# Graph attention with residual norms: the last half blocks' norms moved to VectorE, one residual added through TensorE

## The chip, the cores and the metric

The kernel runs on one core of a Trainium2 chip. A core has TensorE (matrix products, written PE in the profile; PEld is its loading of weights), VectorE (DVE), ScalarE (ACT), GpSimd (POOL) and SyncE (SP), which issues most of the transfers. The metric is the device time of one execution in microseconds (us), as the median of several runs.

## The reference

There are 8 graphs of 2048 nodes with 256 channels, and one 2048 x 2048 adjacency matrix for all. One attention layer with 8 heads of 32 channels is computed, then a feed-forward part, with three layer norms (the two inside have a gain and an offset):

```python
qkv = einsum('fnc,ck->fnk', x, w_qkv); q, k, v = split(qkv, 3)      # 8 heads of 32
scores = where(adj > 0, q @ k.T / sqrt(32), -1e9)
t = softmax(scores) @ v
y = layernorm(x + t, ln1_g, ln1_b)
h = relu(y @ w1 + b1)
z = layernorm(y + h @ w2 + b2, ln2_g, ln2_b)
out = layernorm(x + z)          # over the 256 channels, no gain or offset
```

All of it is in float32. The outputs are 8 x 2048 x 256 numbers.

## The kernel before

**Items.** The work is cut into items (f, qc, g, mb): graph f, a block qc of 512 queries (four to a graph), a group g of four heads, and a block mb of 128 keys. Graphs are the outer loop, then query blocks, the two groups, and 16 key blocks. For each item `scores` does the score products of TensorE (L276) into PSUM and two mask adds of VectorE (L279, operation TENSOR_TENSOR p<-s,mask), `exponentials` one ACTIVATE of ScalarE over 128 x 2048 numbers (L283), and `values` the products with v (L310). `add_up` (L330 to L339) sums the exponentials of the key blocks, partly with adds on GpSimd and partly with accumulating DMAs that GpSimd issues. The loop issues the exponential of item t + 1, the scores of item t + 2 and the values of item t in step t. A score buffer is free for the next product when VectorE has read it; there are three pairs of PSUM banks for scores, and two banks more, one for the values in progress and one for everything else.

**Side work.** Everything else is written as generators that are kept in the list `fill`, each with a start step and a due step. In every step `advance` resumes those that are ready, ordered by due step. `yield n` means: not before n steps from now. `yield BANK` waits for the free PSUM bank, of which there is one a step as long as values are being accumulated, and it is also held back by a credit for TensorE's time. So what a generator issues between two yields lands on every engine's queue at that place of the order. Each engine works through its queue in order.

For one query block the side work is: `denominator` (L382) adds up the four remaining terms with products against `halves`; `outcome` then takes the transposed values (`divide`, L427), multiplies by the reciprocals, adds the input rows x and starts `tail`. `tail` is norm, `feed_forward` (transposes, L575, w1 with L588, w2 with the add L601), norm, gain g2 and offset be2 on GpSimd (L441, L443), the residual of the input, norm, and the output DMA (L449). `norm` takes statistics on VectorE (L348, L349), four small operations on GpSimd (L353 to L357) for the reciprocal deviation rs and the bias nb, and four ACTIVATE on ScalarE (L360).

**The end.** Three query blocks from the end are special. For block NCK - 3 of the last graph the usual form is used with a due step that is nearer. For block NCK - 2 the input rows `xb` lie in SBUF already, and L411 adds them to y on VectorE; everywhere else an accumulating DMA (L414) does that. Its second residual, too, comes from `xb`, to which be2 has been added (L435), as the operand of L443. This block is called the third block or the block in front below. The very last group of heads, ENDING, is worked through in two halves of 256 queries (h = 0 and 1), each with eight items of two key blocks; its score products are L264, its mask adds L268, its values L298 with the copy L303. For each half `closing(h)` is started: five denominator terms (L490; the list `terms` says which sum and the earliest step), the add into dT (L493), transposes, reciprocal (L504), products with it (L522), the input rows (L525), a norm (`half_stats`, L456 to L460, and `half_norm`), transposes, L537, w1 with L545, w2 with the add L555, a second norm, g2 and be2 with the residual (L560, L561), a third norm, and the output DMA (L565). GpSimd computes the residual path beside it (L531, L532). The norm itself is, before the change,

```python
nc.vector.scalar_tensor_tensor(nb, mv[:, :, 0], -1.0, rs, op0=ALU.mult, op1=ALU.mult)
for j in range(2):
    nc.scalar.activation(t[:, j, :], t[:, j, :], AF.Identity, bias=nb[:, j:j + 1], scale=rs[:, j:j + 1])
```

After the last item `advance` is called until `fill` is empty, and the order in which the two closings and the third block's tail alternate comes out of that. A last check of the sums (L971 to L982) follows; on these inputs the branch after it isn't taken.

Of the kernel before, what the change touches and what calls it, by code (L numbers as in the profile page):

```python
# [10 lines left out]
F32 = mybir.dt.float32  # L11
# [4 lines left out]
AF = mybir.ActivationFunctionType  # L16
ALU = mybir.AluOpType
AX = mybir.AxisListType

P = 128  # L20
# [9 lines left out]
BANK, MORE, WAIT, TURNED, ROOM, INPUTS = -1, -2, -3, -4, -5, -10  # L30
# [21 lines left out]
def in_columns(nc, out, lhsT, rhs, start, stop):  # L52
    for r in range(0, P, D):
        nc.tensor.matmul(out[r:r + D], lhsT[:, r:r + D], rhs, start=start, stop=stop)  # L54
# [7 lines left out]
def fast_path(ctx, tc, cst, x, adj, out, RS):  # L62
    nc = tc.nc
    F, N, C = x.shape
    NCK, TPC, MB = N // CH, CH // P, N // P
# [12 lines left out]
    small = ctx.enter_context(tc.tile_pool(name="small", bufs=4))  # L78
# [6 lines left out]
    ident, identb, wqkv, w1s, w2s = cst["ident"], cst["identb"], cst["wqkv"], cst["w1s"], cst["w2s"]  # L85
    state = {"pair": 0, "side": None, "turn": 0, "turned": False, "holder": None, "tails": 0, "credit": 0}

    def columns(out, lhsT, rhs, start, stop):
        state["credit"] -= 4 * out.shape[-1]
        in_columns(nc, out, lhsT, rhs, start, stop)  # L90
# [11 lines left out]
    def bank(dt=F32):  # L102
        shape = [P, CH] if dt == F32 else [P, 2, CH]
        if state["side"] is not None:
            i = 1 - state["side"]
            return ps_x[i].tile(shape, dt, name=f"x{i}")
        i = state["turn"]
        state["turn"] = (i + 1) % 5
        pool = ps_s[i] if i < 3 else ps_x[i - 3]
        return pool.tile(shape, dt, name=f"s{i}" if i < 3 else f"x{i - 3}")  # L110
# [4 lines left out]
    def take(shape, dt):  # L115
        live.pop(0)
        live.append(ld.tile(shape, dt, name="in"))
        return live[-1]
# [245 lines left out]
    def rows(v):  # L364
        return v[:, None, :].to_broadcast([P, TPC, C])
# [35 lines left out]
    def outcome(f, qc):  # L401
        yield ROOM
        state["tails"] += 1
        xin = x[f, qc * CH:(qc + 1) * CH, :].rearrange("(p j) c -> p j c", p=P)
        y = yp.tile([P, TPC, C], F32, name="y")
        begin = items.index((f, qc, 1, LAST)) + SUM + 2
        yield from divide(f, qc, y)
        if (f, qc) == (F - 1, NCK - 2):
            yield 1
            xb = state["xb"]  # L410
            nc.vector.tensor_tensor(y, y, xb, ALU.add)  # L411
            start(begin + 3, tail(f, qc, y, xin, 2, xb), begin + 18)
            return
        nc.gpsimd.dma_start(y, xin, accum_op=ALU.add)  # L414
        if (f, qc) == (F - 1, NCK - 3):
            start(begin + 10, tail(f, qc, y, xin, 2), begin + 18)
        else:
            start(begin + 10, tail(f, qc, y, xin), begin + 26)

    def divide(f, qc, y):  # L420
        rc = RC.pop((f, qc))
        for gg in range(2):
            oT = OT.pop((f, qc, gg))
            yield BANK
            ps = bank()
            transposes(ps, [oT[:, j::TPC] for j in range(TPC)])
            nc.vector.tensor_tensor(y[:, :, gg * P:(gg + 1) * P].rearrange("p j (h d) -> p j h d", d=D),  # L427
                                    ps.rearrange("p (j h d) -> p j h d", h=4, d=D),
                                    rc[:, :, gg::2, None].to_broadcast([P, TPC, 4, D]), ALU.mult)

    def tail(f, qc, y, xin, per=1, xb=None):
        yield from norm(y, per)
        yield from feed_forward(y)
        if xb is not None:
            nc.gpsimd.tensor_tensor(xb, xb, rows(cst["be2r"]), ALU.add)  # L435
        yield 1
        z = y
        yield from norm(z, per if per == 1 else TPC)
        while xb is None and per > 1 and state["now"] % MB not in CALM:
            yield 1  # L440
        nc.gpsimd.tensor_tensor(z, z, rows(cst["g2r"]), ALU.mult)  # L441
        yield 1
        nc.gpsimd.tensor_tensor(z, z, rows(cst["be2r"]) if xb is None else xb, ALU.add)  # L443
        yield 1
        if xb is None:
            nc.gpsimd.dma_start(z, xin, accum_op=ALU.add)
            yield 7 if per == 1 else 10
        yield from norm(z, per)
        nc.sync.dma_start(out[f, qc * CH:(qc + 1) * CH, :].rearrange("(p j) c -> p j c", p=P), z)  # L449
        state["tails"] -= 1  # L450

    def half_stats(t):
        mv = small.tile([P, 2, nc.vector.BN_AGGR_DIM], F32, name="mv")
        for j in range(2):
            st = small.tile([P, nc.vector.BN_STATS_DIM], F32, name="st")
            nc.vector.bn_stats(st, t[:, j, :])  # L456
            nc.vector.bn_aggr(mv[:, j, :], st)
        rs = small.tile([P, 2], F32, name="rs")
        nc.gpsimd.tensor_scalar(rs, mv[:, :, 1], EPS, 1.0, op0=ALU.add, op1=ALU.mult)
        nc.gpsimd.tensor_tensor(rs, rs, cst["mhalf"][:, 0:2], ALU.pow)  # L460
        return mv, rs

    def half_norm(t, mv, rs):
        nb = small.tile([P, 2], F32, name="nb")
        nc.vector.scalar_tensor_tensor(nb, mv[:, :, 0], -1.0, rs, op0=ALU.mult, op1=ALU.mult)
        for j in range(2):
            nc.scalar.activation(t[:, j, :], t[:, j, :], AF.Identity, bias=nb[:, j:j + 1], scale=rs[:, j:j + 1])

    def closing(h):
        f, qc, g = ENDING  # L470
# [4 lines left out]
        def row2(v):  # L475
            return v[:, None, :].to_broadcast([P, 2, C])

        yield BANK
        ps = bank()
        for n, (block, when) in enumerate(terms):  # L480
# [6 lines left out]
            for b in range(2):  # L487
                for i in range(4):
                    r = D * i
                    nc.tensor.matmul(ps[r:r + D, 0:HQ], cst["halves"][:, g, :], term[:, i, b * HQ:(b + 1) * HQ],  # L490
                                     start=(n + b == 0), stop=(n + b == len(terms)))
# [6 lines left out]
        xr, xb = (t[:, own] for t in state["rows"])  # L498
# [27 lines left out]
        found = half_stats(y)  # L526
        if h:
            count(den)
        yield 1
        half_norm(y, *found)  # L530
        nc.gpsimd.tensor_tensor(xr, y, row2(cst["g1r"]), ALU.mult)  # L531
        nc.gpsimd.tensor_tensor(xr, xr, row2(cst["be1b2r"]), ALU.add)  # L532
        yield BANK
        ps = bank()
        transposes(ps, [y[:, j, a * P:(a + 1) * P] for a in range(2) for j in range(2)])
        for a in range(2):
            nc.scalar.activation(yT[:, a, part], ps[:, a * HQ:(a + 1) * HQ], AF.Identity,  # L537
                                 bias=cst["be1c"][:, a:a + 1], scale=cst["g1c"][:, a:a + 1])
        yield 1
        for d in range(2):  # L540
            yield BANK
            ps = bank()
# [5 lines left out]
        ps = bank()  # L548
# [4 lines left out]
                columns(ps[:, j * C:(j + 1) * C], hT[:, d, part][:, j * P:(j + 1) * P], w2s[:, d, :], start=(d == 0), stop=(d == 1))  # L553
        z = y
        nc.vector.tensor_tensor(z, ps.rearrange("p (b c) -> p b c", c=C), xr, ALU.add)  # L555
        found = half_stats(z)
        yield 1
        half_norm(z, *found)
        yield 1
        nc.vector.tensor_tensor(z, z, row2(cst["g2r"]), ALU.mult)  # L560
        nc.vector.tensor_tensor(z, z, xb, ALU.add)  # L561
        found = half_stats(z)
        yield 1
        half_norm(z, *found)
# [41 lines left out]
    def start(t, gen, due):  # L606
        fill.append([t, gen, 1, due])
        fill.sort(key=lambda e: e[3])
# [120 lines left out]
    for t, (f, qc, g, mb) in enumerate(items):  # L729
# [17 lines left out]
        if t == len(items) - MB:  # L747
            xr, xb = state["rows"] = [take([P, TPC, C], F32) for _ in range(2)]
# [23 lines left out]
    t = len(items)  # L772
# [244 lines left out]
```

## Time and profile before

| what | value |
|---|---|
| median of 3 runs | 3167.66 us (3167.57 to 3168.4) |
| profiled execution | 3165.28 us |
| its span, first to last instruction | 3163.5 us |
| granted TensorE clock, mean | 0.995 |
| busy: TensorE, VectorE, ScalarE, GpSimd | 97%, 87%, 77%, 82% |
| L279, mask add 128 x 1024 | 2016 of 1218 ns |
| L283, exponential 128 x 2048 | 1024 of 1910 ns |
| L339, GpSimd's add 128 x 2048 | 378 of 4881 ns |
| L411, the add of `xb` | one of 5009 ns |
| last scores of the last item begin | 3115.66 us |
| last output DMA issued after | 3158.23 us |

Times inside the span are counted from its first instruction. A line of the profile names the engine, the operation and the tiles (output <- inputs), and L with a number is the line of the kernel's file. A bracket at the end of a timeline row gives the time that the engine had been idle, and the instruction that ended this. In the timeline a duration covers an instruction's own latency: neighbours on one engine overlap by about a tenth of a microsecond, so the time from start to start is what counts for sums.

### The profile page before, as it was taken

Reading aid. Unit: us, or ns where it says so; the run is one execution under the profiler, and the core shown is the slowest. Engines: PE = TensorE matmul, PEld = TensorE weight load, DVE = VectorE, ACT = ScalarE, POOL = GpSimd, SP = SyncE. Lnnn points to the kernel's source line nnn. Section 1 sums busy time; section 2 is a strip of 40 time slices with the busy share of each in tenths; the row PEclk is TensorE's granted clock in tenths of the full one; section 3 lists DMA queues with packets and bytes.
Section 4 is the critical chain, followed back from the end, with each engine's and each line's share of the span. In section 5 each row is a group of like instructions: output and inputs, shape, how many; then the busy total and the mean of one; then the engine's idle time right before and its main releaser. Section 6 shows DMA issues by size and latency. Waiting matters only on the chain.

```text
span 3163.5 us, 68998 instructions
## 1 busy us (share of the span) xinstructions
PE 3071.6 (97%) x29220; PEld 969.5 (31%) x29220; DVE 2751.4 (87%) x3138; ACT 2423.8 (77%) x1934; POOL 2589.8 (82%) x1358
## 2 busy tenths in 40 slices
PE   8899999999999999999999999999999999999986
PEld 4222233222332233322333323323233323332223
DVE  4989888998888998888988898888888888889885
ACT  4777777777778877778877878777778777778774
POOL 1768888888888988888888888888889888889885
PEclk9999999999999999999999999999999999999998
DMA  8998888988888988789878888879879888888861
GB/s 255 224 213 187 189 184 182 205 189 192 178 176 202 198 186 182 167 197 218 186 168 187 191 199 192 180 174 204 193 172 205 178 192 193 177 174 167 174 149 42
DMA packets 165467, 586.89 MB, mean 186 GB/s; under 512 B 15360, under 2 KB 84480, under 8 KB 116512
## 3 DMA queue, kind: packets, MB, share of 16 engines
q0 software_dynamic: 63696, 430.60, 69.0%
q1 hardware_dynamic: 100640, 150.50, 14.1%
q8 instruction: 231, 3.78, 0.5%
q10 hardware_dynamic: 816, 1.31, 0.1%
q14 instruction: 84, 0.69, 0.1%
HBM read 146.15 MB, written 37.75 MB: 58 GB/s over the span
## 4 chain that ended last, share of the span: by engine, by line


## 5 line engine op out<-in xcount | busy, mean ns | idle before, releaser
L279 DVE TENSOR_TENSOR p<-s,mask 128x1024 f32<-128x1024 f32 x2016 | 2371.1, 1218 | 302.3 <-PE s L276 170.2
L283 ACT ACTIVATE p<-p 128x2048 f32<-128x2048 f32 x1024 | 1955.8, 1910 | 565.3 <-DVE p L279 458.2
L339 POOL TENSOR_TENSOR p<-p 128x2048 f32<-128x2048 f32 x378 | 1845.1, 4881 | 332.7 <-ACT p L283 332.2
L276 PE MATMUL s<-qT,kT 32*128 32x512 f32 x8064 | 1152.4, 640 | 48.1 <-DVE p L279 44.7
L310 PE MATMUL x<-p,v 128*32 128x512 f32 x8064 | 1075.3, 605 | 3.0 <-ACT oT L314 3.0
L276 PEld LDWEIGHTS s<-qT,kT 32*128 32x128 f32 x8064 | 315.5, 183 | 653.6 <-DVE p L279 627.7
L336 POOL DMA_DIRECT2D p<-p x378 | 406.5, 1076 | 69.7 <-ACT p L283 49.4
L310 PEld LDWEIGHTS x<-p,v 128*32 128x32 f32 x8064 | 158.7, 108 | 768.2 <-issue 303.5
L382 PE MATMUL x<-p,halves 128*32 128x512 f32 x2016 | 261.1, 592 | 0.3 <-ACT turned L575 0.3
L54 PE MATMUL x<-in,wqkv 128*32 128x512 f32 x1888 | 245.6, 592 | 1.5 <-DVE y L170 0.8
L360 ACT ACTIVATE y<-y,nb,rs 128x256 f32<-128x256 f32 x372 | 218.3, 591 | 1.5 <-POOL nb L357 1.4
L348 DVE BATCH_NORM_STATS2 st<-y 128x6 f32<-128x256 f32 x372 | 154.7, 416 | 0.0
L54 PE MATMUL x<-turned,w1s 128*32 128x512 f32 (+1 forms) x1024 | 127.1, 593 | 0.0
L54 PEld LDWEIGHTS x<-wqkv,in 128*32 128x32 f32 x3584 | 102.2, 110 | 62.9 <-issue 54.5
L54 PE MATMUL x<-w2s,hT 128*32 128x256 f32 x2016 | 120.3, 379 | 0.0
L54 PE MATMUL x<-wqkv,in 128*32 128x128 f32 x3584 | 117.1, 273 | 0.0
L382 PEld LDWEIGHTS x<-p,halves 128*32 128x32 f32 x2016 | 65.4, 110 | 149.8 <-issue 147.2
L54 PEld LDWEIGHTS x<-in,wqkv 128*32 128x32 f32 x1888 | 61.1, 110 | 143.4 <-issue 115.1
L354 POOL TENSOR_TENSOR rs<-rs,mhalf 128x4 f32<-128x4 f32 x93 | 96.2, 1035 | 7.7
L441 POOL TENSOR_TENSOR y<-y,g2r 128x1024 f32<-128x1024 f32 x31 | 100.4, 3240 | 0.0
L443 POOL TENSOR_TENSOR y<-y,be2r 128x1024 f32<-128x1024 f32 x30 | 92.1, 3071 | 0.6
L54 PEld LDWEIGHTS x<-w2s,hT 128*32 128x32 f32 x2016 | 65.4, 110 | 68.9 <-issue 35.3
(155 smaller groups left out, 1423.1 us busy)
## 6 DMA issues: line engine op xcount, KB each, us to landing
p<-p POOLq DMA_DIRECT2D x380, 1024.0 KB, 10.1
in<-xd SPq DMA_DIRECT2D x87, 512.0 KB, 8.7
mask<-md SPq DMA_DIRECT2D x248, 128.0 KB, 8.5
y<-in_x_dram POOLq DMA_DIRECT2D x60, 512.0 KB, 9.7
out_dram<-y SPq DMA_DIRECT2D x31, 512.0 KB, 5.9
in<-in_x_dram SPq DMA_DIRECT2D x30, 512.0 KB, 10.3
xd<-in SPq DMA_DIRECT2D x28, 512.0 KB, 8.3
p<-in_adj_dram SPq DMA_DIRECT2D x8, 1024.0 KB, 14.1
```

Of the source, the lines that this page charges most:

```text
L54: nc.tensor.matmul(out[r:r + D], lhsT[:, r:r + D], rhs, start=start, stop=stop)
L276: nc.tensor.matmul(ps2[half][:, j, :], KT[f, mb // TPC, g][r:r + D, (mb % TPC) * P:(mb % TPC + 1) * P], QT[f, qc, g][r:r + D, :], start=Tr ...
L279: nc.vector.tensor_tensor(pt[:, 2 * half:2 * half + 2, :], ps, MK[f, qc, mb // 2][:, mb % 2, None, :].to_broadcast([P, 2, CH]), ALU.add)
L283: nc.scalar.activation(PT[item], PT[item], AF.Exp, scale=1.0 / math.sqrt(D))
L310: nc.tensor.matmul(O[grp][r:r + D, :], V[f, mb // TPC, g][:, mb % TPC, r:r + D], PT[item][:, h, :], start=(mb == 0), stop=(mb == LAST))
L336: nc.gpsimd.dma_start(PT[f, qc, g, chain[0]], PT.pop(item), accum_op=ALU.add)
L339: nc.gpsimd.tensor_tensor(first, first, PT.pop(item), ALU.add)
L348: nc.vector.bn_stats(st, t[:, j, :])
L354: nc.gpsimd.tensor_tensor(rs, rs, cst["mhalf"], ALU.pow)
L360: nc.scalar.activation(t[:, j, :], t[:, j, :], AF.Identity, bias=nb[:, j:j + 1], scale=rs[:, j:j + 1])
L382: nc.tensor.matmul(ps[r:r + D, :], cst["halves"][:, g, :], term[:, h, :], start=(n == 0), stop=(n == len(blocks) - 1))
L441: nc.gpsimd.tensor_tensor(z, z, rows(cst["g2r"]), ALU.mult)
```

## The change

Three things are changed. In `outcome` the input rows of the third block are no longer added by L411: for two halves of the block, TensorE multiplies the identity matrix with two rows' worth of `xb` into a PSUM bank, VectorE adds that bank to y, and `tail` starts at begin + 4 instead of begin + 3. In `tail`, for this block alone, the two `yield 1` around the second GpSimd step (L443) go. In `closing` the norms are done by VectorE alone: `half_norm` becomes one `tensor_scalar` for each of two rows, subtracting the mean and multiplying by rs, without nb; and the second norm is put together with g2 and the residual in two steps for each row, the first of which needs only the mean.

```diff
         if (f, qc) == (F - 1, NCK - 2):
-            yield 1
             xb = state["xb"]
-            nc.vector.tensor_tensor(y, y, xb, ALU.add)
-            start(begin + 3, tail(f, qc, y, xin, 2, xb), begin + 18)
+            for j in range(0, TPC, 2):
+                yield BANK
+                ps = bank()
+                columns(ps, ident, xb[:, j:j + 2, :].rearrange("p j c -> p (j c)"), start=True, stop=True)
+                nc.vector.tensor_tensor(y[:, j:j + 2, :], ps.rearrange("p (j c) -> p j c", c=C), y[:, j:j + 2, :], ALU.add)
+            start(begin + 4, tail(f, qc, y, xin, 2, xb), begin + 18)
             return
...
         nc.gpsimd.tensor_tensor(z, z, rows(cst["g2r"]), ALU.mult)
-        yield 1
+        if xb is None:
+            yield 1
         nc.gpsimd.tensor_tensor(z, z, rows(cst["be2r"]) if xb is None else xb, ALU.add)
-        yield 1
         if xb is None:
+            yield 1
             nc.gpsimd.dma_start(z, xin, accum_op=ALU.add)
...
     def half_norm(t, mv, rs):
-        nb = small.tile([P, 2], F32, name="nb")
-        nc.vector.scalar_tensor_tensor(nb, mv[:, :, 0], -1.0, rs, op0=ALU.mult, op1=ALU.mult)
         for j in range(2):
-            nc.scalar.activation(t[:, j, :], t[:, j, :], AF.Identity, bias=nb[:, j:j + 1], scale=rs[:, j:j + 1])
+            nc.vector.tensor_scalar(t[:, j, :], t[:, j, :], mv[:, j, 0:1], rs[:, j:j + 1], op0=ALU.subtract, op1=ALU.mult)
...
         nc.vector.tensor_tensor(z, ps.rearrange("p (b c) -> p b c", c=C), xr, ALU.add)
-        found = half_stats(z)
-        yield 1
-        half_norm(z, *found)
-        yield 1
-        nc.vector.tensor_tensor(z, z, row2(cst["g2r"]), ALU.mult)
-        nc.vector.tensor_tensor(z, z, xb, ALU.add)
+        mv, rs = half_stats(z)
+        for j in range(2):
+            nc.vector.scalar_tensor_tensor(z[:, j, :], z[:, j, :], mv[:, j, 0:1], cst["g2r"], op0=ALU.subtract, op1=ALU.mult)
+        yield 1
+        for j in range(2):
+            nc.vector.scalar_tensor_tensor(z[:, j, :], z[:, j, :], rs[:, j:j + 1], xb[:, j, :], op0=ALU.mult, op1=ALU.add)
         found = half_stats(z)
         yield 1
         half_norm(z, *found)
```

In the changed file the line numbers are shifted by two or three from `outcome` on: the adds of the identity products are L414 with the products under `in_columns` (L54), `half_norm` is L469, and the two new steps of the second norm are L560 and L563. Where the prediction speaks of rows that both kernels have, it uses the numbers of the kernel before.

## The prediction

> **What bounds the kernel now.** I read the page first. In its busy table TensorE has 97% of the span, and the 40 slices are even up to the last. The two built programs issue the same order on every engine until about 3042 us of the span of 3163.5, so only the last 125 us can differ. The page's chain of waits is empty for this execution, so I read those from the timeline, engine by engine, then the stage table of that stretch for the granted clock.
>
> First the third residual (`state["xb"]`, L411), which the change replaces. Timeline, columns: start us, duration us, engine, line and operation, idle before it and what ended that:
>
> ```profile
> 3042.45 0.68 DVE L427 TENSOR_TENSOR y<-x,rc 128x512 f32<-128x512 f32 x1
> 3043.05 2.34 DVE L279 TENSOR_TENSOR p<-s,mask 128x1024 f32<-128x1024 f32 x2
> 3044.71 4.52 POOL L339 TENSOR_TENSOR p<-p 128x2048 f32<-128x2048 f32 x1 [0.28 <-ACT p L283]
> 3045.31 5.01 DVE L411 TENSOR_TENSOR y<-y,in 128x1024 f32<-128x1024 f32 x1
> 3050.24 2.34 DVE L279 TENSOR_TENSOR p<-s,mask 128x1024 f32<-128x1024 f32 x2
> 3051.51 2.09 PE L276 MATMUL s<-qT,kT 32*128 32x512 f32 x8 [5.06 <-DVE p L279]
> ```
>
> An add of 1024 elements per partition takes 5.01 us, where two mask adds of the same size (L279) take 2.34 together. GpSimd's add started 0.6 us before it and ended at 3049.23: VectorE waited that long and then worked 1.1 us. TensorE stood 5.06 us, and its next matmuls took 2.09 us instead of the usual 1.14.
>
> Second, the closing, from the last denominators (L490, ended about 3125.3) to the last norm:
>
> ```profile
> 3125.44 0.42 DVE L493 TENSOR_TENSOR dT<-x,dT 128x256 f32<-128x256 f32 x1 [5.80 <-PE x L490]
> 3125.78 0.42 DVE L348 BATCH_NORM_STATS2 st<-y 128x6 f32<-128x256 f32 x1
> ...
> 3127.91 0.23 DVE L504 RECIPROCAL rc<-x 128x16 f32<-128x16 f32 x1
> ...
> 3134.09 1.09 ACT L467 ACTIVATE y<-y,nb,rs 128x256 f32<-128x256 f32 x2 [10.01 <-DVE nb L465]
> ...
> 3139.06 3.64 PE L54 MATMUL x<-turned,w1s 128*32 128x256 f32 x32
> ...
> 3146.69 0.69 DVE L555 TENSOR_TENSOR y<-s,in 128x512 f32<-128x512 f32 x1 [11.43 <-PE s L54]
> ...
> 3158.23 1.09 ACT L467 ACTIVATE y<-y,nb,rs 128x256 f32<-128x256 f32 x2 [0.19 <-DVE nb L465]
> ```
>
> VectorE idles 5.80 us before the last denominators, then does the statistics of the third block (L348, four at 0.53 with L349) while the reciprocal waits. The first half's norm runs on ScalarE at 3134.09, the second's only at 3137.09 because two L537 stand between; w1 starts at 3139.06 behind the second half's transposes. The stage table adds that w1 begins at half clock (column PEclk, the third from the right):
>
> ```profile
> 3139.00:3141.00 2.00, 2.00 (x21) 0.99 (x24) 0.00 (x0) 1.02 (x2) 1.92 (x3) 0.50 0.00 0
> 3143.00:3145.00 2.00, 2.00 (x40) 1.06 (x36) 0.00 (x0) 0.85 (x3) 0.00 (x0) 0.92 0.00 0
> ```
>
> **What the Trainium skill says.** "SBUF — State Buffer", section "SBUF: two separate sides": VectorE operations with two SBUF inputs, or in a 2-port mode, share a port pair with GpSimd; whoever starts first has it for a whole instruction. L411 agrees (4 us of waiting). It also excuses L279, whose one operand is in PSUM, and so the new add from PSUM. "VectorE: DVE Perf Modes", "The perf-mode tier table": an fp32 `tensor_scalar` within SBUF yields two results a cycle, `tensor_tensor` one. The trace's only SBUF case is L696, 1024 elements in 0.686 us: at 0.96 GHz 0.533 plus 0.153 fixed, so 256 elements are estimated at 0.29. "TensorE: Matmul & The Clock Gate", Part 1: the clock halves after an idle window of about 3.4 us and needs a busy one to return. The trace agrees, with 2.28 us of idling at 3010 already enough once.
>
> **The change, part by part.**
>
> *1. Identity products.* Removed: L411, 4.93 us from its start to the next pair. Added on TensorE: two products of four matmuls, each like a term of L382 (a slot with one takes 2.93 to 2.94), beside VectorE's slots of 2.87 (pair 2.27 plus a 0.60 step as at L427): nearly hidden. Added on VectorE: two adds at 0.60 by that row. The balance is 3.7 us, and about 0.8 of the slow-clock matmuls after it goes too, so VectorE's pair for the first ending item falls from 3069.3 to about 3064.8, 4.4 earlier. ScalarE is late next. From the exponential of the eighteenth-last item on (3061.3 after the change) it has five exponentials (1.87 each, start to start), four pairs of L360 (1.02), one L314 (0.5), two L575 (0.71): 15.4 us, ending 3076.7 to 3077.4; before, the same exponential ended at 3080.34. `values` (L298) wait for it, TensorE is in order, and the PSUM bank of the first denominator waits for the second L575. So 3.3 us reach the items, not 4.4. GpSimd keeps up: it idled 4.71 us before the add at 3054.75. Bounds: 1.5 (ScalarE's queue longer by one more pair and a copy) to 4.4.
>
> *2. One slot later.* Two products take two slots, and `tail` starts at begin + 4, so all of the third block's tail and, behind it for banks, the last denominators come one slot later. In the built order the ending half's five terms (L490) all follow the last `values`, where before only two did; the four L360 of the tail's second norm come ahead of the last exponential instead of the last but one. Last scores 3115.66 − 3.3 = 3112.3; exponential of the item before ends 3115.0; L360 2.06; last exponential to 3119.0; `values` 0.86; five terms 4.3: 3124.2 against 3125.3. So 1.2 of the 3.3 is left; 2.1 is given back. Beside it: L441 and L443 (2.38 each, two `yield`s fewer) end at 3122.0, the four statistics (2.15) at 3124.2. They now stand **ahead** of the last denominators' add on VectorE, whose queue is behind them: it balances by a hair, and every us that L443 is late costs one.
>
> *3. First norms.* From the end of the denominators: transposes of both halves (all ready), add, reciprocal, two L522 (0.79), L525 (0.73), two statistics (1.09) for each half, then the norm. With rows' start-to-start times: first half's reciprocal 0.7 after the denominators (before 2.6: the 2.1 of statistics are gone from here), second half's statistics end at 6.5. Two `tensor_scalar` (0.55) replace the `nb` step and two ACTIVATE (0.13 + 1.09), and no L537 stands between the halves. rs of the second half is ready at 7.7 (GpSimd has the third block's four small operations, 1.85, in front); transposes, and w1 starts at 9.65, before 13.76: 4.1 less. From w1 to L555 stays 7.63, clock apart. Bounds 3.0 (`tensor_scalar` as dear as ACTIVATE, 0.59) and 4.6.
>
> *4. Last norms.* From L555 to the last norm's end, 12.63 before. Now: L555 0.73, statistics 1.09, two L560 (nearest row L348's 0.40, also 256 elements), second half the same with 0.2 of the flag's steps, then twice two L563 (0.40 each) and statistics, then 1.05 for rs and 0.55: 10.9. Gain 1.75, bounds 1.0 and 2.2. The output DMA keeps its 4.2 us to the end.
>
> *5. Clock and port.* TensorE's break before the transposes of y shrinks from 7.6 to about 5 us, still slow, but its busy stretch starts earlier relative to w1: of 4.2 us at half clock I expect 2.4, 0.9 saved (0 to 2). The wait for the last exponential, 2.2 us, may halve the clock: 1.7 at four in ten, 0.6 lost. Eight `tensor_scalar` and eight two-input steps can meet GpSimd's L531 and L532 (1.27 each) or its small steps; I take 0.6, half an L531.
>
> Removed ScalarE work (L467, 6.5 us) costs nothing elsewhere. SP's three output DMAs keep their order; GpSimd's DMA issue L332 moves ahead of the four norm steps, harmless.
>
> Sum: −1.2 − 4.1 − 1.75 − 0.9 + 0.6 + 0.6 = −6.75. The profiled execution took 3165.28 (span 3163.5 plus 1.8), so 3158.5; the median is 2.4 above it, so the median goes to 3160.9.
>
> **Rivals.**
>
> *A, the late slots eat it.* ScalarE's queue lets through only 2 us, the clock halves in the wait of part 2: −6.75 + 1.3 + 1.1 = −4.3, 3163.3. For it: ScalarE is 10.00 of 10.00 busy in 3070 to 3080. Against: TensorE's slots are full afterwards. Chance 0.22.
>
> *B, all of it arrives.* 4.4 through the items, clock back early: −6.75 − 1.1 − 1.1 − 0.6 = −9.5, 3158.2. Chance 0.14.
>
> *C, slower by the port.* One mechanism: in the closing, VectorE's sixteen new SBUF-only steps lose the port to GpSimd each time. GpSimd works about 12 us there (four of 1.27, six pairs of 0.19 and 0.71, the third block's 1.6). From 7.3 us of such waits the gain is gone, and all 12 with the rs they delay in turn give up to +7: 3167 to 3175. For it: L411 lost 4 us that way. Against: most of GpSimd's steps wait for VectorE's, so the two alternate, and at 3154.4 it was GpSimd that waited. Chance 0.05.
>
> *D, nothing arrives,* because L411's stall is filled by others anyway. The 5.06 us of TensorE speak against it; 3167, chance 0.03.
>
> **How the numbers follow.** The main sum has 0.56; its bounds give 3158.5 to 3163. A measurement here tells about 0.2% (6.3 us) from no change, so the line is 3161.3, close to the forecast. Main: somewhat over half below the line plus an even spill, 0.39 of 0.56; B 0.14, A 0.02: faster 0.55. Within: 0.17 + 0.20 + 0.01 + 0.03: 0.41. Slower: 0.04 from C. The range takes in A and B: 3157.0 to 3164.8.
>
> **What would show it.** Right: no VectorE step near 5 us around 3045 and no 5 us break of L276; ScalarE without gaps from about 3061 to 3077; last scores near 3112.3; five terms after the last `values`, ending near 3124; statistics finished within half a us of them; w1 near 3133.8; span near 3157. Wrong: the scores' end earlier or later by over 1.5 us (part 1), a break of VectorE ahead of the statistics with the denominators already done (part 2), steps of L469 or L563 above 0.6 us (port).

## The result, and the profile after

The changed kernel takes 3160.89 us (median of 12 runs, 3158.64 to 3166.98) against 3168.2 of the kernel before beside it (12 runs, 3165.89 to 3170.08): ratio 0.9979, 95% interval 0.9971 to 0.9987. The forecast was 3160.9. The profiled execution took 3162.05 us, its span is 3160.2.

The same code in front of the change differs by a few us from one execution to the next (at 54 us of the span the changed kernel is already 1.7 late, at 3041 it is 3.5). All places below are therefore counted from one common point: the start of the last score product (L276) ahead of the third residual's slot, at 3041.53 before and 3045.04 after.

| event, us from the common point | before | after | difference | its share of the change |
|---|---|---|---|---|
| first ending scores (L264) | 26.48 | 21.97 | -4.51 | |
| last ending scores | 74.14 | 70.37 | -3.77 | |
| first transposes of the closing (L95), the denominators' end | 83.77 | 82.09 | -1.68 | -1.68 |
| first product of w1 (L54) | 97.53 | 93.90 | -3.63 | -1.95 |
| first result of w2 taken (L555, now L557) | 105.16 | 100.65 | -4.51 | -0.88 |
| end of the last norm | 117.79 | 111.55 | -6.24 | -1.73 |
| end of the span | 121.97 | 115.16 | -6.81 | -0.57 |

First the place where L411 took 5.01 us. Timeline of the changed kernel, columns as before:

```profile
3045.97 0.68 DVE L430 TENSOR_TENSOR y<-x,rc 128x512 f32<-128x512 f32 x1
3046.56 2.35 DVE L279 TENSOR_TENSOR p<-s,mask 128x1024 f32<-128x1024 f32 x2
3048.24 4.59 POOL L339 TENSOR_TENSOR p<-p 128x2048 f32<-128x2048 f32 x1 [0.28 <-ACT p L283]
3048.83 0.68 DVE L414 TENSOR_TENSOR y<-x,y 128x512 f32<-128x512 f32 x1
3050.89 1.14 PE L276 MATMUL s<-qT,kT 32*128 32x512 f32 x8
3051.69 0.68 DVE L414 TENSOR_TENSOR y<-x,y 128x512 f32<-128x512 f32 x1
```

GpSimd's add runs from 3048.24 as before, and the new add (L414) beside it takes 0.68 us: its one operand is in PSUM. TensorE's break of 5 us and the half-clocked product after it are gone.

Second, the end of the denominators and the first norms:

```profile
3121.81 1.07 PE L298 MATMUL x<-p,v 128*32 128x256 f32 x16 [1.66 <-ACT p L283]
3122.47 2.38 POOL L447 TENSOR_TENSOR y<-y,in 128x1024 f32<-128x1024 f32 x1
3122.70 4.50 PE L492 MATMUL s<-p,halves 128*32 128x256 f32 x80
3124.88 0.43 DVE L348 BATCH_NORM_STATS2 st<-y 128x6 f32<-128x256 f32 x1 [4.24 <-POOL y L447]
3127.27 0.42 DVE L495 TENSOR_TENSOR dT<-s,dT 128x256 f32<-128x256 f32 x1 [0.15 <-PE s L492]
...
3133.76 0.73 DVE L469 TENSOR_SCALAR y<-y,mv,rs 128x256 f32<-128x256 f32 x2
3134.62 0.71 POOL L464 TENSOR_TENSOR rs<-rs,mhalf 128x2 f32<-128x2 f32 x1
3135.30 1.26 POOL L533 TENSOR_TENSOR in<-y,g1r 128x512 f32<-128x512 f32 x1
3135.36 2.69 DVE L469 TENSOR_SCALAR y<-y,mv,rs 128x256 f32<-128x256 f32 x2 [0.87 <-POOL rs L464]
3136.64 1.27 POOL L534 TENSOR_TENSOR in<-in,be1b2r 128x512 f32<-128x512 f32 x1
3138.94 1.08 PE L54 MATMUL x<-turned,w1s 128*32 128x256 f32 x8
```

All five terms (80 products, L492) follow the last `values`. VectorE waits 4.24 us for the third block's sum (L447), does its statistics, and is done 0.15 us ahead of the denominators. The first half's norm takes 0.73 us; the second half's, the same two instructions, 2.69.

The granted clock (third column from the right) returns during w1, as before, but earlier: at 3141.5, which is 2.5 us after w1 starts; before, at 3143.3 and 4.2 us after it.

```profile
3139.00:3141.00 2.00, 2.00 (x21) 0.93 (x24) 0.00 (x0) 1.08 (x3) 1.67 (x2) 0.50 0.00 0
3143.00:3145.00 2.00, 2.00 (x44) 1.14 (x40) 0.00 (x0) 2.00 (x6) 0.00 (x0) 1.00 0.03 8
```

### The profile page after: what moved, and what is told of

It is laid out like the page before. It is cut to its first block, busy times and chain, and to the rows that moved or that the text cites. A ratio compares the mean times of both kernels' runs of the same rounds, so it can differ in the third digit from the quotient of the medians.

```text
span 3160.2 us, 69015 instructions
## 1 busy us (share of the span) xinstructions
PE 3071.8 (97%) x29236; PEld 969.9 (31%) x29236; DVE 2753.2 (87%) x3145; ACT 2416.9 (76%) x1922; POOL 2590.1 (82%) x1358
## 4 chain that ended last, share of the span: by engine, by line
PE 79%; DVE 9%; issue 1%; ACT 1%; POOL 0%; DMA 0%; DVEq 0%; ACTq 0%; POOLq 0%
PE s L276 29%; PE x L310 25%; PE x L54 16%; DVE p L279 6%; PE x L382 6%; PE x L95 3%; DVE st L348 1%; DVE dT L388 1%; PE s L264 0%; ACT p L283 0%; DVE y L430 0%; PE x L298 0%; DMA p<-p 0%; DVE p L268 0%; POOL p L339 0%
## 5 line engine op out<-in xcount | busy, mean ns | idle before, releaser
L276 PE MATMUL s<-qT,kT 32*128 32x512 f32 x8064 | 1151.5, 640 | 43.4 <-DVE p L279 40.1
L276 PEld LDWEIGHTS s<-qT,kT 32*128 32x128 f32 x8064 | 315.4, 183 | 648.2 <-DVE p L279 622.3
L54 PE MATMUL x<-in,wqkv 128*32 128x512 f32 x1888 | 245.6, 592 | 1.5 <-DVE y L170 0.8
L54 PE MATMUL x<-turned,w1s 128*32 128x512 f32 (+1 forms) x1008 | 125.4, 593 | 0.8 <-ACT in L194 0.8
L54 PE MATMUL x<-w2s,hT 128*32 128x256 f32 x2048 | 122.0, 379 | 0.0
L54 PEld LDWEIGHTS x<-wqkv,in 128*32 128x32 f32 x3584 | 102.2, 110 | 62.9 <-issue 54.5
L54 PE MATMUL x<-wqkv,in 128*32 128x128 f32 x3584 | 117.1, 273 | 0.0
L54 PEld LDWEIGHTS x<-in,wqkv 128*32 128x32 f32 x1888 | 61.1, 110 | 143.4 <-issue 115.1
L447 POOL TENSOR_TENSOR y<-y,be2r 128x1024 f32<-128x1024 f32 x30 | 92.1, 3071 | 0.6
L54 PEld LDWEIGHTS x<-w2s,hT 128*32 128x32 f32 x2048 | 66.4, 110 | 69.7 <-issue 35.3
## 6 DMA issues: line engine op xcount, KB each, us to landing
in<-in_x_dram SPq DMA_DIRECT2D x30, 512.0 KB, 10.2
```

Source lines behind the costliest of these rows:

```text
L276: nc.tensor.matmul(ps2[half][:, j, :], KT[f, mb // TPC, g][r:r + D, (mb % TPC) * P:(mb % TPC + 1) * P], QT[f, qc, g][r:r + D, :], start=Tr ...
```

## The experiments

Theory: each part works where the prediction put it, and the one large loss is that GpSimd's two residual steps (L533, L534) hold the shared port while the second half's norm waits. The rivals were that the residual's gain or the norms alone carry the change, or that the second pair is slow for another reason. The columns give us from the common point; the last is the ratio to the kernel before beside it, with its 95% interval.

| kernel | denominators' end | w1 starts | w2 result taken | span ends | ratio |
|---|---|---|---|---|---|
| before | 83.77 | 97.53 | 105.16 | 121.97 | |
| changed | 82.09 | 93.90 | 100.65 | 115.16 | 0.9979 (0.9971 to 0.9987) |
| changed, second comparison | 82.09 | 93.91 | 101.13 | 115.68 | 0.9979 (0.9971 to 0.9987) |
| identity products alone | 82.09 | 94.93 | 101.52 | 119.00 | 0.9995 (0.9986 to 1.0003) |
| closing's norms alone | 83.77 | 95.31 | 102.34 | 117.07 | 0.9983 (0.9975 to 0.9991) |
| tail's yields alone | 83.93 | 96.27 | 103.91 | 121.00 | 0.9995 (0.9987 to 1.0004) |
| residual steps in the other order | 82.07 | 91.92 | 99.63 | 114.14 | 0.9975 (0.9965 to 0.9985) |
| statistics later | 82.08 | 93.33 | 100.45 | 116.77 | 0.9986 (0.9979 to 0.9993) |
| add in SBUF one slot earlier | 78.40 | 90.74 | 98.67 | 115.91 | 0.9980 (0.9973 to 0.9987) |
| early add, norms, yields out, order | 83.42 | 93.56 | 101.10 | 115.83 | 0.9976 (0.9968 to 0.9984) |
| the same, 24 idle transposes | 83.23 | 93.35 | 100.74 | 115.47 | 0.9979 (0.9973 to 0.9986) |
| early add, norms, order | 78.42 | 88.56 | 95.03 | 109.80 | 0.9958 (0.9945 to 0.9972) |
| the same, 44 idle transposes | 78.42 | 88.19 | 93.70 | 108.43 | 0.9960 (0.9946 to 0.9973) |

### One part at a time

Identity products alone (the first hunk of the diff, nothing else):

> The kernel before with the third residual by identity products and the tail one slot later, and nothing else; both yields of the tail and the closing's norms on ScalarE stay. Times are counted from the start of the last score product before the residual's slot, where both kernels still agree. Theory (part 1 and 2 of the prediction): the first ending scores come 4.4 us earlier (+22.0 instead of +26.5), the last ending scores 3.3 to 3.8 earlier (about +70.4 instead of +74.1), and five denominator terms behind the last values leave 1.2 to 1.7 of it at the end of the denominators (about +82.1 instead of +83.8). The closing behind it is as long as before within 0.7 us, because the statistics of the third block only move from in front of the first half to between the halves: the span falls by 1.2 to 2.2 us. Rival: the residual's gain reaches the end whole, since TensorE was the bound: the span falls by 3.5 or more. Second rival: ScalarE's queue takes all of it, the span falls by less than 0.5.

Measured: first ending scores +21.97, last +70.38, denominators' end +82.09, the three of the changed kernel to 0.01 us. So all that happens ahead of the closing comes from this part. The span falls by 3.0, more than the 1.2 to 2.2 expected: 1.7 at the denominators as forecast, but the closing, too, is 1.3 shorter where at most 0.7 was allowed (0.9 up to w1, 1.0 from w1 to the result of w2 by the clock, 0.7 lost after the last norm). By time alone (0.9995) the part can't be told from no change.

The closing's norms alone (hunks of `half_norm` and of the last norms):

> The changed kernel with the residual's add in SBUF and the tail's two yields put back: only the closing's norms are on VectorE alone. Theory: the scores and the end of the denominators stay as before (+74.1 and +83.8 us from the last common score product, within 0.7). From the end of the denominators to w1 13.76 us before: the statistics of the third block (2.15) still stand in front of the first half; the norms save the nb step and the ACTIVATEs, 1 to 2 us, unless GpSimd's products of the residual take the port from the second half's pair again (L467 pair of the second half over 2 us). From w1's evacuated result (L555 of before) to the last norm's end 10.9 instead of 12.6. In all 3 us off the span, between 2.3 and 4.5. Rival: the closing alone carries the change, 5.5 us or more. Second rival: on VectorE the norms lose the port each time, the span falls by less than 1.

Measured: nothing moves ahead of the closing, w1 starts 11.54 us behind the denominators' end (13.76 before), the last norm ends 10.90 us after the first result of w2 as forecast, and the span falls by 4.9, beyond the 2.3 to 4.5 expected: from w1 to the result of w2 it takes 0.6 less than before, and the norms save 2.2 where 1 to 2 was expected. Here both pairs take the short time, since four small GpSimd steps of the third block (from 3135.56) stand between the second rs and the residual product (L529):

```profile
3135.51 0.73 DVE L465 TENSOR_SCALAR y<-y,mv,rs 128x256 f32<-128x256 f32 x2 [0.58 <-POOL rs L460]
3135.56 0.19 POOL L353 TENSOR_SCALAR rs<-mv 128x4 f32<-128x4 f32 x1
3137.37 1.27 POOL L529 TENSOR_TENSOR in<-y,g1r 128x512 f32<-128x512 f32 x1
```

The tail's yields alone:

```diff
-        yield 1
+        if xb is None:
+            yield 1
         nc.gpsimd.tensor_tensor(z, z, rows(cst["be2r"]) if xb is None else xb, ALU.add)
-        yield 1
         if xb is None:
+            yield 1
```

> The kernel before with the two yields of the third block's tail (the steps with xb) taken out, and nothing else. The product and the sum on GpSimd already follow each other without a gap before, so their times stay; what moves is the place of the block's four statistics on VectorE, from behind the last denominators' add to ahead of it. Theory: GpSimd's sum ends about 3122.6, the statistics (2.15 us) fill VectorE's idle 5.8 us and end 0.5 us ahead of the denominators, and all of the closing moves up by 2.1: w1 starts 11.6 us after the closing's first transposes instead of 13.8, the span falls by 2.1. Half of part 3's gain is then this line. Rival: the four small GpSimd steps of the third block and its norm on ScalarE now get in front of the first half's, and half or more of the 2.1 is lost: less than 1 us.

Measured: the statistics do stand ahead of the denominators, yet w1 comes only 1.4 us earlier relative to them (12.34 against 13.76), the span falls by 1.0, and the time (0.9995) tells nothing. The 2.1 don't arrive whole because the statistics had hidden another wait. In this order the half with h = 1 comes first, and its sums are the ones just finished: the add (L494), TensorE's transposes of dT and the reciprocal follow one another, and VectorE stands 0.60 us in between. So the reciprocal starts 1.17 us behind the denominators' end where it started 2.61 behind it before. That is 1.44, and the rest of the chain up to w1 keeps it:

```profile
3129.97 0.42 DVE L494 TENSOR_TENSOR dT<-x,dT 128x256 f32<-128x256 f32 x1 [0.86 <-PE x L491]
3130.45 0.75 PE L95 MATMUL x<-ident,dT 128*128 128x128 f32 x4
3131.00 0.26 DVE L505 RECIPROCAL rc<-x 128x16 f32<-128x16 f32 x1 [0.60 <-PE x L95]
```

In the changed kernel the half with h = 0 comes first. Its sums were added up 7 us earlier (3120.22), and its reciprocal starts 0.54 us behind the denominators' end.

Alone the three parts take 3.0, 4.9 and 1.0 off the span, together 8.9; in one kernel they take 6.8. The granted clock has a share in all these numbers, so the starts of w1 compare better: alone 2.60, 2.22 and 1.26 earlier, together 6.1; in one kernel 3.63. Of the 2.5 that is missing 2.0 is the slow pair of the changed kernel, which none of the three has alone (next section); the rest was not traced.

### The slow pair

```diff
-        nc.gpsimd.tensor_tensor(xr, y, row2(cst["g1r"]), ALU.mult)
-        nc.gpsimd.tensor_tensor(xr, xr, row2(cst["be1b2r"]), ALU.add)
+        def residual():
+            nc.gpsimd.tensor_tensor(xr, y, row2(cst["g1r"]), ALU.mult)
+            nc.gpsimd.tensor_tensor(xr, xr, row2(cst["be1b2r"]), ALU.add)
+
+        if h:
+            residual()
...
             nc.scalar.activation(hT[:, d, part], ps[:, 0:HQ], AF.Relu, bias=cst["b1s"][:, d:d + 1], scale=1.0)
+        if not h:
+            residual()
         yield 1
```

The second place is behind the products of w1 in `closing`.

> The changed kernel with one thing moved: GpSimd forms the first half's second residual (L533 and L534, 1.27 us each) behind the second half's instead of as soon as the first half's norm is done. Nothing reads it before L557, 12 us later. Theory: in the changed kernel the second half's pair of L469 took 2.69 instead of 0.73 us because those two GpSimd steps held the port one after the other; with GpSimd idle there the pair takes 0.7 to 0.8, w1 starts 2.0 us earlier (10 us behind the first transposes of the closing instead of 11.8) and the span is 2.0 shorter than the changed kernel's, unless half-clocked matmuls return up to 0.7 of it. Rival: the second pair is slow for another reason (its own operands, rs late on GpSimd): the pair stays over 2 us and the span moves by less than 0.5.

Measured: the second pair (the upper row is the first half's) takes 0.73 us, and w1 starts 9.85 us behind the denominators' end instead of 11.81:

```profile
3135.46 0.73 DVE L469 TENSOR_SCALAR y<-y,mv,rs 128x256 f32<-128x256 f32 x2
3136.32 0.71 POOL L464 TENSOR_TENSOR rs<-rs,mhalf 128x2 f32<-128x2 f32 x1
3137.06 0.73 DVE L469 TENSOR_SCALAR y<-y,mv,rs 128x256 f32<-128x256 f32 x2 [0.88 <-POOL rs L464]
3137.88 1.27 POOL L534 TENSOR_TENSOR in<-y,g1r 128x512 f32<-128x512 f32 x1 [0.85 <-DVE y L469]
```

Same instructions, same data, another order on GpSimd: 1.96 us. Of these 1.0 reaches the end; from w1 to the first result of w2 it takes 7.71 instead of 6.75. The clock comes back at the same place in both kernels, 96.4 us from the common point, so w1, which starts 2.0 earlier, runs at half clock 4.4 us instead of 2.5. By time alone this kernel isn't told from the changed one.

The changed kernel in a second profile:

> The changed kernel once more, on the chip of the two runs beside it. Expected: 6 to 8 us below before; its last common score product to the end within 0.5 of the 115.2 us of its first profile; the second half's pair of L469 again at 2.7 us, since GpSimd's L533 is due at the same moment each time (if it is 0.7 here, the collision is a matter of chance and not of the order).

Measured: the pair takes 2.69 us again and L533 starts 0.06 ahead of it again, so the collision comes with the order and not by chance. The end is at +115.68, 0.52 from the first profile and just outside the 0.5 expected: w1 to the result of w2 took 7.22, not 6.75, since the clock came back 1.0 us later, at +97.4.

### The statistics behind both norms

```diff
         if xb is None:
             yield 1
             nc.gpsimd.dma_start(z, xin, accum_op=ALU.add)
             yield 7 if per == 1 else 10
-        yield from norm(z, per)
+        else:
+            yield 5
+        yield from norm(z, per if xb is None else TPC)
```

The third block's last norm so starts five steps later, and takes its four rows at once instead of two and two.

> The changed kernel with the third block's last norm (statistics, small GpSimd steps, norm, output) put behind both halves' first norms, into the 7 us in which VectorE waits for w1 and w2. Theory: the statistics cost nothing where they stood (they end with the denominators), but the four small GpSimd steps of that block (0.56, 1.01, 0.20 and 0.20 us) stood between the two halves' rs: without them the second rs is ready before the first half's pair ends, its pair runs right behind it, ahead of GpSimd's residual products, and the collision of 2 us goes as well: w1 starts 9.5 to 9.9 us after the first transposes instead of 11.8, the span is 1 to 2.3 shorter than the changed kernel's. Rival: the block's statistics, norm and output now delay the last norms or the last output by as much; the span moves by less than 0.5 either way, or is longer.

Measured: the second rs is ready earlier, but the pair still takes 2.69 us: GpSimd's product starts 0.07 us ahead of it.

```profile
3137.05 0.70 POOL L466 TENSOR_TENSOR rs<-rs,mhalf 128x2 f32<-128x2 f32 x1
3137.72 1.27 POOL L535 TENSOR_TENSOR in<-y,g1r 128x512 f32<-128x512 f32 x1
3137.79 2.69 DVE L471 TENSOR_SCALAR y<-y,mv,rs 128x256 f32<-128x256 f32 x2 [0.32 <-POOL rs L466]
```

The expected order failed: the pair waits for rs, GpSimd makes it, and its own next instruction is the product. That product starts 0.67 us after the start of the step that makes rs, VectorE's pair 0.74 after it. The third block's output now is issued last (3159.84), 5.4 us lie between the last norm and the end instead of 3.6, and the kernel isn't faster than the changed one.

### The residual without identity products

```diff
-            yield 1
             xb = state["xb"]
             nc.vector.tensor_tensor(y, y, xb, ALU.add)
             start(begin + 3, tail(f, qc, y, xin, 2, xb), begin + 18)
```

> The kernel before with one line taken out: the yield ahead of the third residual's add in SBUF. VectorE so does the same 1024-element add one slot earlier, ahead of the mask adds of that slot, where GpSimd is between two of its own. Theory: L411 took 5.01 us only because GpSimd's add started 0.6 us before it and held the shared port for 4 us; the work of it is 1.1 us. Then it takes 1.1 to 1.7 us here, TensorE's break of 5 us goes, the first ending scores come 3 to 3.9 us earlier, with no slot given to identity products and no term moved behind the last values, so that the end of the denominators gains 2 to 3.5 and the span as much. Rival: the add is slow by itself or meets the next GpSimd add as well: again about 5 us, the span within 1 us of before.

Measured: the same add (now L410) takes 1.54 us.

```profile
3038.93 4.56 POOL L339 TENSOR_TENSOR p<-p 128x2048 f32<-128x2048 f32 x1 [1.90 <-ACT p L283]
3042.32 0.68 DVE L426 TENSOR_TENSOR y<-x,rc 128x512 f32<-128x512 f32 x1
3043.03 1.54 DVE L410 TENSOR_TENSOR y<-y,in 128x1024 f32<-128x1024 f32 x1
3044.58 4.53 POOL L339 TENSOR_TENSOR p<-p 128x2048 f32<-128x2048 f32 x1 [0.28 <-ACT p L283]
```

GpSimd's add ends at 3043.49, 0.46 after VectorE's start, and 1.54 - 0.46 is 1.08 of work, the same as in L411's 5.01 us (3045.31 to 3049.23 of waiting). Once VectorE came 0.6 us after the start of GpSimd's add and once 0.46 before its end, and each time it waited for that end: GpSimd held the port for the whole instruction, as the Trainium skill has it ("SBUF — State Buffer", "SBUF: two separate sides"). These rows don't show the reverse, GpSimd waiting for VectorE: its next add starts at 3044.58, just as VectorE's ends, but 3.19 us from the common point, where it starts in the kernel before as well (3.18). So the add fits between two GpSimd adds with nothing to spare; in the five kernels that have it there it took 1.53 to 1.55 us.

One deleted line gives 5.4 us at the denominators' end, more than the 2 to 3.5 expected, where the identity products give 1.7. It brings less to the first ending scores (+23.17 against +21.97), but the extra slots aren't taken: the last `values` start at +75.67 instead of +76.77, and only 2.73 us later the denominators are done instead of 5.32, because three of the five terms precede the last `values`.

### The two gains together

The changed kernel with the early add in place of the identity products (and `begin + 3`), and GpSimd's other order. The tail's yields are out. In the kernels without the extra slots the closing with h = 1 comes first, so the condition is the reverse of the one shown above:

```diff
+        if not h:
+            residual()
...
+        if h:
+            residual()
```

> The changed kernel with the third residual added in SBUF one slot earlier (as in the experiment on the add) instead of by identity products, and GpSimd's two residual steps of the half that comes first put behind the other half's. Theory: the two gains add, since one lies ahead of the last denominators and one behind. First transposes of the closing about 78.4 us after the last common score product (82.1 in the changed kernel), w1 9.9 us behind them, 7 to 7.7 to the first evacuated result, 10.9 to the last norm's end, 3.6 to the end: 110 to 110.5 against 115.2 of the changed kernel and 122.0 before: 11.5 us below before, about 3157 with a median of 3168.5 for before. Rival: without the identity products' slot the yields taken out put the statistics in front of a score item's mask, or the third block's steps meet the closing, and the gain over the changed kernel is under 2 us.

The rival came true. Without the extra slot the yields' removal puts the third block's statistics ahead of mask adds that feed the last scores; VectorE waits for L443 and TensorE behind it:

```profile
3116.70 0.43 DVE L348 BATCH_NORM_STATS2 st<-y 128x6 f32<-128x256 f32 x1 [3.64 <-POOL y L443]
3117.79 2.32 DVE L268 TENSOR_TENSOR p<-s,mask 128x1024 f32<-128x1024 f32 x2
3119.04 2.01 PE L264 MATMUL s<-qT,kT 32*128 32x256 f32 x16 [3.59 <-DVE p L268]
```

The denominators end at +83.42 instead of +78.40: the whole 5 us of the early add are gone. The same kernel with 24 transposes that nobody reads, ahead of the wait for y (24 is six times four):

```diff
         if h:
             rc, den = turned_sums()
+        else:
+            yield BANK
+            idle = bank()
+            for n in range(6):
+                transposes(idle, [OT[f, qc, gg][:, part][:, j::2] for gg in range(2) for j in range(2)])
```

> The kernel of the run beside it (early add, residual steps moved) with 24 transposes of data already there, into a PSUM bank that nobody reads, behind the closing's last transposes on TensorE: they fill most of its break ahead of the transposes of y. Theory: w1 and what follows runs at half clock because of that break; with TensorE busy the four w1 groups take half as long, and w1's start to the first evacuated result falls from 7 to 7.7 to about 6.2 to 6.5 us: the span 0.6 to 1.3 shorter than that of the run beside it. Rival: the transposes are in front of work that is ready, or the clock falls all the same: no gain, or a loss up to 1 us.

Little came of it: TensorE's break shrinks from 5.80 to 3.01 us, the clock halves in it all the same (full until 3136, half at 3137), and w1 to w2's result takes 7.39 instead of 7.54.

With the tail's yields kept, that is without the hunk of `tail`:

```diff
-        if xb is None:
-            yield 1
+        yield 1
         nc.gpsimd.tensor_tensor(z, z, rows(cst["be2r"]) if xb is None else xb, ALU.add)
+        yield 1
         if xb is None:
-            yield 1
```

> The kernel before with three things: the third residual's add in SBUF one slot earlier (the yield ahead of it gone), the changed kernel's norms on VectorE in the closing, and GpSimd's two residual steps of the half that comes first put behind the other half's. Both yields of the third block's tail stay, so that its statistics come behind the last mask adds of the scores, as in the experiment with the add alone, and not ahead of them. Theory: the gains ahead of and behind the last denominators add: first transposes of the closing 78.4 us after the last common score product, w1 10.1 behind, first evacuated result 7.5 later, last norm's end 10.9, end 3.8: 110.7 us, against 115.2 of the changed kernel and 122.0 before; so 11.3 below before and 4.5 below the changed kernel. Rival: the earlier denominators find GpSimd still at the third block's tail, so that the closing is longer by 2 us or more and most of the addition is lost.

Measured: +109.80 at the end, 12.2 below before; median 3156.5 (5 runs) where before had 3169.13 and the changed kernel 3163.14 on the same chip. Both gains arrive: the early add's in full at the denominators (+78.42), and w1 starts 10.14 behind them (9.85 with the identity products and the other order). How much of the second is GpSimd's order isn't shown, as the early add and the norms were not run together without it. The ratio's interval only touches that of the changed kernel (0.9972 and 0.9971). This is the version to keep.

And with the idle transposes, `range(11)` instead of `range(6)`:

> The kernel of the run beside it with 44 transposes instead of none (24 in the earlier run left a break of 3.0 us) behind the closing's last transposes on TensorE, into a bank that nobody reads. 24 filled 2.9 us, so 44 fill 5.3 of the 5.8 us. Theory: the clock halved in the remaining 3 us before; with half a us left it stays at full speed, the two y transposes and w1 run at full clock and w1's start to the first evacuated result falls from 7.5 to about 6.2, the span by 1.3 to 1.6. Rival: the clock halves all the same, or the transposes stand in the way of those of y: no gain.

Measured: with 44 transposes TensorE's break is 0.61 us, the clock stays full through w1, and w1 to w2's result takes 5.51 us instead of 6.47:

```profile
3131.00:3133.00 2.00, 2.00 (x38) 1.20 (x40) 0.00 (x0) 1.83 (x4) 1.92 (x2) 1.00 0.00 0
```

The span ends at +108.43, 1.37 earlier as expected: 0.96 from w1 on and 0.37 ahead of it, where the transposes of y run at full clock (0.78 us for four instead of 1.22 and 1.14). The time doesn't tell the two apart (3156.94 against 3156.5), so the trace alone shows this gain.

## Why the prediction was right

- **Identity products: right.** -4.4 forecast for VectorE's first pair of the ending items, -4.50 measured, and -4.51 for the first ending scores. ScalarE has the instructions that were listed, with one gap of 0.38 us, and the exponential that ended at 3080.34 before ends 3.58 us earlier (3.0 to 3.6 forecast). At the last scores 3.77 is left where 3.3 was forecast.
- **One slot later: right in its mechanism.** 2.1 to be given back, 3.77 - 1.68 = 2.09 measured. The early add shows it from the other side: without the slots it is only 0.35 ahead of the changed kernel at the last scores, and 3.69 at the denominators' end. The statistics end 0.15 us ahead of the denominators, where "by a hair" was written.
- **First norms: the sum missed by 2.** 9.65 from the denominators to w1 was forecast, 11.81 measured. With the collision taken away it is 9.85, so the other steps were right in sum and the loss belongs to the next item.
- **Port: the term that was mis-sized.** "I take 0.6, half an L531" treated the meeting as partial and likely. In all three profiles with this order it is there, and whole: GpSimd's product stands right behind the rs that VectorE waits for, and the second of VectorE's two instructions meets the next GpSimd step as well. It costs 1.96 us, over three times the term. The prediction's own sign for this, steps of L469 above 0.6 us, came true: two of them took 2.69 together. The rival C named this loss, but spread it over sixteen steps: fourteen of them took 0.36 or 0.43 us each in the traces, two paid. And it didn't see what follows from its own item 2: with the statistics ahead of the denominators, the third block's small GpSimd steps no longer stand between the second rs and the product, as they do with the norms alone.
- **Last norms: right in sum.** 10.9 forecast and 10.90 measured. Up to the last statistics it took 8.9 us, where the listed steps make 9.2; the pairs of L560 and L563 take 0.76 to 0.79 from start to start, so 0.40 a step held. The last rs and the norm took 2.0 instead of 1.6. The pair of L469 took 0.73 instead of 0.55: the estimate of 0.29 a step was made from L696, which reads int32 and writes bf16, and not from a float32 step.
- **Clock: right in the first profile, by its place.** -0.9 forecast from 2.4 us of w1 at half clock; 2.5 us and -0.88 in the first profile, and -0.41 in the second. The last section shows what decides it. The 0.6 set aside for a halving in the wait for the last exponential wasn't paid: the wait was 1.66 us and the clock stayed full.
- **The end.** 4.2 us from the last norm to the end were to stay, 3.61 were measured. It goes with the engine of the last norm: 4.18 to 4.86 in the four kernels that have it on ScalarE, 3.61 to 3.87 in eight that have it on VectorE (5.43 in the one whose third block is put out last). Why is not shown.

The total of -6.75 against -6.81 is closer than its parts: the port cost 1.4 more than its term and the first norms gained 0.2 less; 1.1 at the denominators (0.5 more gain, 0.6 not lost) and 0.6 at the end made up for it. That the median fits to 0.01 us is luck too: the second comparison gives 6.0 us between the medians (3163.14 against 3169.13), the first 7.3.

## What to carry to other kernels

When two VectorE and GpSimd steps in SBUF can meet, look at the order of their queues, not at their shares of busy time. Here a GpSimd step that stood right behind the value VectorE was waiting for won in all three profiles, and moving it behind the wait gave 1.96 us at that place. Before work is moved to another engine to get around a long step, try the same step one slot earlier or later; here that gave more than the identity products, because these took slots that the last terms then missed. A change of place that is good with one order of the side work can cost all of its gain with another, as the tail's yields did. And what is gained ahead of a stretch at half clock may be lost in it: the 1.96 us became 1.0.

## What was not expected of the hardware

- Deciding on the port by 0.06 us: L533 started 0.06 (twice) and 0.07 us ahead of VectorE's pair, and held it for two whole instructions, 1.26 and 1.27 us, with one VectorE step in between (TensorE's transposes of y came as one at 3136.85 and three at 3138.11). GpSimd's small steps wait in their turn: in the changed kernel L353, which takes 0.19 us in the kernel before, took 0.56 beside L527 of VectorE (3131.80 to 3132.49, two operands in SBUF), and L463 and L464 took 0.33 and 0.83 beside L560, against 0.19 and 0.71 at the first half's norm.
- The clock changes only on a grid of 3.41 us. In the kernel before it changes at 3013.60, 3017.02, 3051.14, 3054.56, 3129.66 and 3143.30 us: 1, 10, 1, 22 and 4 times 3.41 us apart (from stage tables with a row for each us; a value between 0.50 and 1.00 tells where in its row the change lies). From 2990 to 3150 us the changes in each of the 13 profiles are whole multiples of 3.41 us apart. In the closing:

| kernel | half clock from, us from the common point | full again | length |
|---|---|---|---|
| before | 88.1 | 101.8 | 13.6, four times 3.41 |
| changed | 86.2 | 96.4 | 10.2, three times |
| changed, second profile | 87.1 | 97.4 | 10.2, three times |
| residual steps in the other order | 86.1 | 96.4 | 10.2, three times |
| early add, norms, order | 83.7 | 90.5 | 6.8, twice |

- Cut into such stretches of 3.41 us, the same part of the 13 profiles also shows what halves the clock: it went to half after every stretch at full clock in which TensorE stood 1.99 us or more, and stayed full after every one with 1.77 us or less. It came back only after stretches with at least 2.99 us of work. So a break counts by how much of it falls into one stretch. One of 2.28 us (3010 in the kernel before) and one of 3.0 (24 transposes) were enough; one of 1.66 and one of 0.61 (44 transposes) were not. And half clock began 2.2 us after the start of a break in one kernel (yields out, early add) and 5.1 in another (early add alone).
- Where the grid lies against the kernel differs between executions: by 1.0 us between the two profiles of the changed kernel. That much more of w1 at half clock costs half as much, the 0.5 us by which the two differ from w1 to the result of w2. The Trainium skill ("TensorE: Matmul & The Clock Gate", Part 1) gives an idle window of about 3.4 us and calls it free-running. The length and the free place agree with these traces; that the window need not be idle throughout is what they add.
